# A later planned landing for the convolutions' row copies and for the preparation's read-back tile, in a four-layer state-space and attention kernel

## The chip, the cores and the metric

The kernel runs as one program on one core of a Trainium2 chip. The metric is the device time of one execution in microseconds, lower is better. A core has five engines with a queue of instructions each: TensorE (PE in the profile, its weight loads PEld), VectorE (DVE), ScalarE (ACT), GpSimd (POOL) and SyncE (SP), which here issues all DMAs. Each engine works through its queue in the order in which the program wrote it, and waits at an instruction until what it needs is there.

## The reference

Four layers on images of 64 x 64 positions with 128 channels, batch 4, all in float32.

- Layer 0 splits the channels. The left half goes through 3x3 convolutions (`c1_w`, `c2_w`) and a 1x1. The right half goes through a projection, a depthwise 3x3 convolution with SiLU, and a selective scan over four directions, 128 inner channels and 16 states. Both halves are joined by a 1x1 convolution and added to the input.
- Layer 1 is a layer norm, a projection, a depthwise 3x3 with SiLU, a selective scan with 256 inner channels (two tiles of 128), a norm, a gate, a projection, and a two-layer perceptron with GELU.
- Layer 2 is a gated message over the 3x3 neighbours, layer 3 a 7x7 neighbourhood attention with 4 heads.

The scan is the heart of layers 0 and 1:

```
xs  = four orderings of the image (rows, columns, both reversed)
dts, Bs, Cs = split(x_proj @ xs);  delta = softplus(dt_w @ dts + dt_b)
h   = exp(delta * A) * h + (delta * u) * B      # for each of 16 states
y   = sum over states of h * C, plus D * xs
```

## The kernel before

**Units.** The scans of layers 0 and 1 are cut into 3072 units in a row (4 images of layer 0 with one channel tile, 4 images of layer 1 with two; 256 units a task; 16 units make a step, which is 1024 positions of one direction). A unit holds 8 channels by 16 states on 128 partitions. For one unit SP loads `h` from the DRAM tile `dud` (512 KB, 10 units ahead, L443), PE spreads delta over the states into the PSUM tile `da` and ACT takes its exponential (`decay`, L459), and DVE runs the scan (L476). DVE also multiplies by B for two units at a time, POOL multiplies by C (L457), and PE sums over the states (`add_up`, L557). `da` has two buffers, `h` nine pairs.

**Preparation.** `Scans.prepare` (L339) makes a step's delta, `dud`, B and C, starting 28 units ahead. For a first channel tile PE computes the projection into `xd`, and SP stores it to `xdd`. For the second channel tile of layer 1 (64 of 192 steps) the projection is the same, so `xd` is read back from `xdd` with two DMAs (L378). Then come two pairs of matmul from `xd` and ACT work (L391 on), exponential, logarithm, four operations on POOL, two casts on ACT, the store of `dud`, 12 copies `dp<-parts` and the load of `repC`.

**Side work.** `Side` does all that lies around the scans: `pre0` and `pre1` (projections and the depthwise convolution), `convs`, `post0` and `post1` (output stages). The depthwise convolution (`depthwise`, L813) works in 8 pieces; a piece's rows are three DMAs into one of two `pad` tiles, started when the piece before has issued its first third of matmuls. `conv` (L850) loads two halves of the image at its start and uses them in order. Each DMA group comes with a memset of the image's border on POOL. Both are loaded through `halves` (L801), which notes a time of landing.

**The planner.** Preparation and side work are generators that yield after every small piece, with the engines that the next piece needs and, where it needs a DMA, the planned time of its landing. The program is written out unit by unit (`Scans.run`, L584). At each unit the planner's clock is the unit's number times 3.6 us (`UNIT`), and a lane's next piece is written into the engines' queues if `Lane.fits` (L188) says so:

```python
            start = max(plan.at[kind], self.ready)
            ...
            if start + USUAL[what] > plan.now + UNIT + SLACK[kind] + more:
                return False
```

`ready` is the landing time, `USUAL` is 1.4 us for PE and `SLACK` 1.2. `more` is 0.06 us for each credit that side work has saved up (at most 50; it earns at least 0.83 a unit, more when a deadline is near). A preparation piece that has fallen 4 units behind is written without asking, as is side work whose deadline is reached. Nothing of this is time on the chip: it only sets the order in the queues. Spare time on PE is filled with matmuls on zeros (`fill`, L559).

**What the change touches.** `ROWS_LANDING` is read in `halves`, for the depthwise rows and the convolutions' rows alike:

```python
        def start(n):
            pad = self.pads[n % 2]
            load(pad, n)
            tiles.append((pad, self.nc.now + ROWS_LANDING))
```

`LANDING` is read for the read-back (L379), for the store of `xd` before `repC` (L373), for the fetches of chunks and for the reuse of stored tiles.

Of the kernel before, what the change touches and what calls it, by code (L numbers as in the profile page):

```python
# [36 lines left out]
def image(t):  # L37
    return t.rearrange("p (r w) -> p r w", w=HW)
# [74 lines left out]
SLACK = dict(PE=1.2, ACT=2.2, POOL=3.0)  # L113
LANDING = 10.0
FOUR_LANDING = 14.0
ROWS_LANDING = 18.0


class Plan:
# [22 lines left out]
    def post(self, chain, issue, due=0.0):  # L142

        if self.running:
            self.posted.append((chain, max(self.done, due), issue))
        else:
            issue()
# [78 lines left out]
class ScanWeights:  # L226
# [27 lines left out]
    def load(self):  # L254

        nct, most = self.nct, max(TILES)
        tile = self.pool.tile([P, most * ND * (H + P)], F32, name="xpdt", tag="xpdt", bufs=1)
        self.xp = tile[:, 0 : nct * ND * H].rearrange("p (t k h) -> p t k h", t=nct, k=ND)
        at = most * ND * H
        self.dtw = tile[:, at : at + ND * nct * P].rearrange("p (k c) -> p k c", k=ND)  # L260
        self.nc.sync.dma_start(out=self.xp, in_=self.d_xp)
        for i in range(HALVES):
            self.nc.sync.dma_start(out=self.dtw[i * H : (i + 1) * H], in_=self.d_dtw)
# [22 lines left out]
class Scans:  # L286
# [19 lines left out]
    @staticmethod  # L306
    def half(i):
        return slice(i * T, (i + 1) * T)
# [30 lines left out]
    def prepare(self, t, step):  # L339

        nc, W, half, post = self.plan, t.W, self.half, self.plan.post
        begin = self.plan.now
        k, c = t.steps[step]
        R = W.rank
        rows = R + 2 * NS
        if t.first is None:
            yield "PE" if W.nct > 1 else "PE ACT"

        xd = self.xds[step % 2]
        if t.first is None:  # L350
            xdd = t.xdd[step] = self.dram.tile(
                [rows, TS], F32, name="xdd", tag=f"xdd{W.layer}", bufs=(4, 2 * len(t.steps))[W.layer]
            )
            ps = self.bank()
            for ti in range(W.nct):
                for i in range(HALVES):
                    nc.tensor.matmul(
                        image(ps[i * H : (i + 1) * H, :]),
                        W.xp[:, ti, k, :],
                        self.view(t.xc[ti], k, c, i, HALVES),  # L360
                        start=ti == 0,
                        stop=ti == W.nct - 1,
                    )
                if ti + 1 < W.nct:
                    yield "PE ACT" if ti + 2 == W.nct else "PE"
            nc.scalar.copy(xd, ps)

            def store_xd():
                for i in range(HALVES):
                    nc.sync.dma_start(out=xdd[:, half(i)], in_=xd[i * H : i * H + rows, :])  # L370

            post("prep", store_xd)
            ready = max(self.plan.done, self.plan.now) + LANDING  # L373
            yield "PE ACT"
        else:
            xdd, ready = t.first.xdd[step], begin
            for i in range(HALVES):
                nc.sync.dma_start(out=xd[i * H : i * H + rows, :], in_=xdd[:, half(i)])  # L378
            yield "PE ACT", self.plan.now + LANDING  # L379
        out = t.prepared[step] = {"xd": xd}  # L380

        def repeat():
            out["C"] = self.tile("repC", 2)
            src = bass.AP(xdd.tensor, xdd.offset + (R + NS) * TS, [[TS, NS], [0, 8], [1, TS]])
            nc.sync.dma_start(out=out["C"], in_=src)

        post("rep", repeat, max(begin + 15 * UNIT, ready))

        bias = W.dtb[:, k, t.ct : t.ct + 1]
        delta, low = self.tile("delta", 1), self.tile("low", 1)  # L390
        for i in range(HALVES):  # L391
            ps = self.bank()
            nc.tensor.matmul(
                ps,
                W.dtw[i * H : (i + 1) * H, k, t.ct * P : (t.ct + 1) * P],
                xd[i * H : (i + 1) * H, :],
                start=True,
                stop=True,
            )
            nc.scalar.activation(low[:, half(i)], ps, AF.Abs, bias=bias)  # L400
            nc.scalar.activation(delta[:, half(i)], ps, AF.Relu, bias=bias)
            yield "PE ACT" if i + 1 < HALVES else "ACT"
        nc.scalar.activation(low, low, AF.Exp, scale=-1.0)
        yield "ACT"
        nc.scalar.activation(low, low, AF.Ln, bias=1.0)
        yield "POOL"
        nc.gpsimd.tensor_add(delta, delta, low)
        yield "ACT POOL"
        parts = self.tile("parts", 1, shape=(P, 3, TS), dtype=BF16)
        nc.scalar.copy(parts[:, 0, :], delta)  # L410
        nc.gpsimd.tensor_mul(image(low), image(delta), self.view(t.xc[t.ct], k, c, 0, 1))
        yield "POOL"
        t.x_done = step == len(t.steps) - 1
        dud = out["du"] = self.dram.tile([P, TS], F32, name="dud", tag="dud", bufs=3)
        post("prep", lambda: nc.sync.dma_start(out=dud, in_=low))
        nc.gpsimd.tensor_sub(delta, delta, parts[:, 0, :])
        yield "ACT"
        nc.scalar.copy(parts[:, 1, :], delta)
        yield "POOL"
        nc.gpsimd.tensor_sub(parts[:, 2, :], delta, parts[:, 1, :])  # L420


        def own(part, j):
            if j == part == 0:
                out["delta"] = self.dps[step % 2]
            nc.sync.dma_start(
                out=out["delta"][32 * part : 32 * part + 32, j, :], in_=parts[32 * j : 32 * j + 32, part, :]
            )

        for i in range(12):  # L430
            j, part = divmod(i, 3)
            post("rep", lambda part=part, j=j: own(part, j), begin + (11 + 0.5 * i) * UNIT)
        yield ""
# [221 lines left out]
class Side:  # L655
# [145 lines left out]
    def halves(self, load):  # L801
# [3 lines left out]
# [5 lines that stand above are left out]
# [1399 lines left out]
```

## Time and profile before

| | us |
|---|---|
| median of 3 runs | 13472.44 |
| lowest, highest | 13461.69, 13475.99 |
| the profiled execution | 13484.91 |
| its span, first to last instruction | 13483.1 |
| stretch of the scans (207 to 11213) | 11006 |
| behind the scans (layers 2 and 3) | 2270 |

The profile is of one execution. Its page gives the busy time of each engine, the span in 40 slices, the DMA queues, and the costliest groups of instructions, each with the idle time of its engine just before it and who ended that. Further views give who waited for whom (total, times, longest), the busy times in a stretch, and the instructions in order of time. `L102` is the planner's wrapper, through which all of the preparation's and side work's instructions go, so these are told apart by the tile they write: `ms` is the one PSUM bank of preparation and side work, `pad` the convolutions' rows, `xd` the preparation's tile. The granted TensorE clock is 0.902 of full speed over the span.

### The profile page before, as it was taken

The page shows a single profiled execution, that of the slowest core. Times are in us where ns is not written, and L with a number is a line of the kernel's source. Part 1 is how long each engine was busy: PE and PEld are TensorE (multiplying, and loading weights), DVE is VectorE, ACT ScalarE, POOL GpSimd, SP SyncE. Part 2 cuts the span into 40 slices and gives each one's busy share as a digit, 9 for nine tenths or more (in the row PEclk, how much of TensorE's full clock was granted, in tenths as well). Part 3 has the DMA queues.
Part 4 walks back from the last instruction along what each step waited for, and adds up shares of the span by engine and source line. Part 5 has one row for each costly group of instructions (what it writes and reads, how often), then busy time and mean ns, then how long its engine had stood idle before and what let it go on. Part 6 is the DMA issues. An engine that isn't in the chain of part 4 may idle for free. (4 is left out here: it accounts for less than half of the span.)

```text
span 13483.1 us, 129941 instructions
## 1 busy us (share of the span) xinstructions
PE 9508.7 (71%) x41730; PEld 2802.6 (21%) x42299; DVE 11700.5 (87%) x6988; ACT 7918.1 (59%) x10594; POOL 9716.6 (72%) x3218
## 2 busy tenths in 40 slices
PE   5776777667667776767766677677777676665788
PEld 1111111111111111111111111122112122111455
DVE  4998999989999889989999999999999992677555
ACT  3666556655665556655665555555555554655577
POOL 3887788878887778778888888888888883345200
PEclk8888999989898889989999899999999988877899
DMA  6888888898888888998889888888888882344200
GB/s 157 215 211 219 222 212 214 223 219 219 198 227 206 208 208 211 221 216 215 204 218 220 219 196 199 200 197 213 202 201 201 197 194 73 84 99 104 65 20 17
DMA packets 877394, 2476.31 MB, mean 184 GB/s; under 512 B 142495, under 2 KB 164135, under 8 KB 868519
## 3 DMA queue, kind: packets, MB, share of 16 engines
q1 hardware_dynamic: 876711, 2467.95, 74.0%
q8 instruction: 337, 5.52, 0.2%
q14 instruction: 346, 2.83, 0.1%
HBM read 2044.11 MB, written 272.37 MB: 172 GB/s over the span
## 5 line engine op out<-in xcount | busy, mean ns | idle before, releaser
L457 POOL TENSOR_TENSOR h<-h,repC 128x2048 f32<-128x2048 f32 x1536 | 6953.0, 4532 | 1536.4 <-ACT state L494 1199.7
L476 DVE TENSOR_TENSOR_SCAN h<-da,state,h 128x1024 f32<-128x1024 f32 x2304 | 5302.8, 2338 | 390.3 <-ACT da L467 270.9
L467 ACT ACTIVATE da<-da,av 128x1024 f32<-128x1024 f32 x3072 | 3338.7, 1088 | 3187.2 <-PE da L465 2847.7
L457 DVE TENSOR_TENSOR h<-h,B 128x2048 f32<-128x2048 f32 x1536 | 3474.6, 2262 | 282.7 <-DMA h<-dud 192.0
L465 PE MATMUL da<-dp,spread 128*128 128x512 bf16 x5753 | 1915.1, 411 | 2253.8 <-DVE h L476 2188.2
L557 PE MATMUL yps<-h,gather 128*32 128x512 f32 x12288 | 1866.2, 683 | 17.6 <-issue 3.8
L476 DVE TENSOR_TENSOR_SCAN h<-da,h 128x1024 f32<-128x1024 f32 x768 | 1722.2, 2279 | 128.0 <-ACT da L467 89.8
L562 PE MATMUL yps<-ones,nothing 128*128 128x512 bf16 x4943 | 1438.4, 403 | 32.9 <-issue 28.1
L465 PEld LDWEIGHTS <-spread 128*128 128x128 bf16 x6144 | 553.0, 101 | 4176.2 <-issue 3656.9
L102 ACT ACT_TABLE_LOAD x600 | 769.8, 1283 | 18.3 <-DMA xcd<-o 5.0
L562 PEld LDWEIGHTS <-nothing 128*128 128x128 bf16 x5121 | 457.0, 101 | 1413.1 <-issue 1092.3
L102 PE MATMUL ms<-d,wts 128*128 128x512 f32 (+3 forms) x900 | 547.5, 717 | 253.8 <-POOL d L102 106.4
L102 POOL TENSOR_TENSOR delta<-delta,low 128x1024 f32<-128x1024 f32 x192 | 451.8, 2353 | 312.2 <-ACT low L102 231.0
L102 ACT CAST parts<-delta 128x1024 bf16<-128x1024 f32 x384 | 400.7, 1044 | 440.4 <-POOL delta L102 415.1
L1919 POOL COPY wide_total<-total 128x128 f32<-128x128 f32 x128 | 37.6, 294 | 831.7 <-DVE total L1917 650.8
L102 PE MATMUL ms<-xd,xpdt 64*128 64x512 f32 x768 | 470.3, 694 | 231.6 <-ACT delta L102 82.4
L540 PE MATMUL yps<-y,ident 128*128 128x512 f32 x576 | 483.9, 928 | 78.2 <-ACT y L574 73.7
L102 POOL TENSOR_TENSOR low<-delta,xc 128x1024 f32<-128x1024 f32 x192 | 503.3, 2622 | 8.9
L1475 ACT ACTIVATE hid<-hid,relb 128x1024 f32<-128x1024 f32 x288 | 322.8, 1146 | 271.2 <-DVE hid L1470 271.0
L1888 ACT ACTIVATE s<-s,least 128x512 f32<-128x512 f32 x512 | 372.2, 727 | 178.9 <-DVE least L1875 178.9
L1875 DVE CUSTOM_DVE_ANT_0 s<-sps,bias 128x512 f32<-128x512 f32 x512 | 323.5, 687 | 173.6 <-PE sps L1864 165.0
L1577 POOL TENSOR_TENSOR acc<-acc,part 128x1024 f32<-128x1024 f32 x120 | 309.4, 2584 | 221.3 <-DVE part L1571 134.5
(291 smaller groups left out, 11191.4 us busy)
## 6 DMA issues: line engine op xcount, KB each, us to landing
h<-dud SPq DMA_DIRECT2D x3072, 512.0 KB
dp<-parts SPq DMA_DIRECT2D x2304, 64.0 KB
repC<-xdd SPq DMA_DIRECT2D x192, 512.0 KB
dud<-low SPq DMA_DIRECT2D x192, 512.0 KB
spread<-gd SPq DMA_DIRECT2D x72, 1024.0 KB
pad<-xid SPq DMA_DIRECT2D x192, 256.0 KB
szd<-o SPq DMA_DIRECT2D x96, 256.0 KB
xcd<-o SPq DMA_DIRECT2D x96, 256.0 KB
```

Source lines behind the costliest of these rows:

```text
L102: return call(*args, **kw)
L457: engine.tensor_mul(pair, pair, t.prepared[step][name].unsqueeze(1).to_broadcast([P, 2, TS]))
L465: self.nc.tensor.matmul(da[:, cols], self.C.spread[:, jj, :], dp[:, j, cols], start=True, stop=True)
L467: self.nc.scalar.activation(da, da, AF.Exp, scale=t.W.a[:, at : at + 1])
L476: nc.vector.tensor_tensor_scan(h[:, way], da[:, way], h[:, way], 0.0 if step % NSTEP == 0 else t.states[step - 1][:, u % NG : u % NG + 1], ...
L540: self.nc.tensor.matmul(self.like_part(yps, k), self.C.ident, self.part(t.y, k, c, b), start=True, stop=False)
L557: self.nc.tensor.matmul(out, self.C.gather[jj], rhs, start=False, stop=jj == 3)
L562: self.nc.tensor.matmul(self.live["yps"], self.C.nothing, self.C.ones16, start=False, stop=False, skip_group_check=True)
L1475: nc.scalar.activation(hid, hid, AF.Gelu, bias=self.relb[:, m, t : t + 1])
L1577: (nc.vector if alone and pair else nc.gpsimd).tensor_add(acc, acc, part)
L1875: self.nc.vector.tensor_tensor_reduce(out=self.live["s", n][:, h, :], in0=self.live["sps", n][:, h, :], in1=self.bias[case][:, h, :], scal ...
L1888: self.nc.scalar.activation(s, s, AF.Exp, scale=-1.0, bias=self.live["least", n][:, h : h + 1], accum_out=self.live["total", n][:, h : h + 1],
```

## The change

The planned landing of the convolutions' rows goes from 18 to 27 us after they are issued, and the planned landing of the read-back `xd` gets a constant of its own, 16 us instead of the common 10. What is computed, in which instructions and on which engine, stays as it is; the places of side work and preparation in the queues change, and with them the number of filling matmuls.

```diff
@@ -113,7 +113,8 @@
 SLACK = dict(PE=1.2, ACT=2.2, POOL=3.0)
 LANDING = 10.0
 FOUR_LANDING = 14.0
-ROWS_LANDING = 18.0
+ROWS_LANDING = 27.0
+AGAIN_LANDING = 16.0
 
 
 class Plan:
@@ -376,7 +377,7 @@
             xdd, ready = t.first.xdd[step], begin
             for i in range(HALVES):
                 nc.sync.dma_start(out=xd[i * H : i * H + rows, :], in_=xdd[:, half(i)])
-            yield "PE ACT", self.plan.now + LANDING
+            yield "PE ACT", self.plan.now + AGAIN_LANDING
         out = t.prepared[step] = {"xd": xd}
```

## The prediction

> **What bounds the kernel now.** I read the busy shares first, then the stretch with the scans alone, then DVE's waits and PE's waits in that stretch, then the timeline of one stall.
>
> ```profile
> PE 9508.7 (71%) x41730; PEld 2802.6 (21%) x42299; DVE 11700.5 (87%) x6988; ACT 7918.1 (59%) x10594; POOL 9716.6 (72%) x3218
> ```
>
> ```profile
> 207.00:11213.00 11006.00, 7779.81 (x30865) 2012.66 (x31437) 10390.05 (x4619) 6472.52 (x8005) 9055.94 (x2732) 0.91 0.85 210
> ```
>
> The columns of the second are length, then busy time of PE, PEld, DVE, ACT, POOL, then clock, DMA share and GB/s. The 3072 scan units take 11006 of 13483 us, 3.58 us each. DVE is busy 10390 us of it (94%), POOL 9056 (82%), PE 7780 (71%). So DVE bounds this stretch, and what can be won without touching DVE's own work is its idle time, 616 us. Gaps under 0.15 us make up 152 us of it (the pipeline's own); 464 us are real waits.
>
> ```profile
> DVE h L476 <- ACT da L467: 360.7, 221, 10.9
> DVE h L457 <- issue: 61.4, 30, 15.2
> DVE h L457 <- PE B L502: 15.6, 13, 5.3
> ```
>
> Columns: total us, times, longest. A scan waits for its decay factors `da`, which ACT makes from a PE matmul. What made PE late is in PE's own waits of the same stretch:
>
> ```profile
> PE da L465 <- DVE h L476: 2188.2, 1303, 10.6
> PE ms L102 <- DMA pad<-xid: 104.7, 21, 11.0
> PE ms L102 <- DMA xd<-xdd: 54.1, 13, 10.6
> PE ms L102 <- DMA pad<-ld: 45.6, 6, 13.8
> PE ms L102 <- DMA dp<-parts: 4.4, 2, 2.9
> ```
>
> The first row is PE waiting for DVE to free a `da` bank, which is harmless. The other four are side or preparation matmuls (`ms`) standing in PE's queue before their tile has landed. The two rows named `dp` are tap matmuls too. In all 208.8 us in 42 waits. While PE stands there, the `da` matmuls behind it wait:
>
> ```profile
> 2976.10 3.73 SPq L799 DMA_DIRECT2D pad<-ld  x4
> ...
> 2993.74 3.66 PE L102 MATMUL ms<-pad,wts 128*64 128x512 f32 x8 [13.80 <-DMA pad<-ld]
> ...
> 2998.40 1.09 ACT L467 ACTIVATE da<-da,av 128x1024 f32<-128x1024 f32 x1 [16.11 <-remote]
> ...
> 2999.53 2.29 DVE L457 TENSOR_TENSOR h<-h,B 128x2048 f32<-128x2048 f32 x1 [15.23 <-issue]
> ```
>
> The convolution's rows are issued at 2976, PE stands 13.8 us until they land, ACT's `da` is 16 us late, DVE loses 15.2 us. Of each such PE wait I added up DVE's gaps (over 0.15 us) in the 12 us after it: pads 149 us of DVE idle after 155 us of PE waits (0.96), `xd` read-backs 43.5 after 54.1 (0.80). So 193 us of DVE's 464 hang on these two landings, and DVE, being the bound, gets them back one for one.
>
> **The change, part by part.** No instruction's work changes; two constants move where the planner puts steps in the queues. A step enters a queue when its start is no later than now + 3.6 + 1.2 - 1.4 us for PE, up to 3 us more with credit. For rows 18 - 3.4 = 14.6 us gives 4 units at least, 27 - 3.4 = 23.6 gives 7, or 6 with credit. For the read-back 10 - 3.4 = 6.6 gives 2 units, 16 - 3.4 = 12.6 gives 4.
>
> *Rows of the convolutions (104 loads beside the scans).* Working the planner's arithmetic through both programs, the tap stands behind its load by 4 units (33 depthwise loads), 5 (17), 6 (17), 7 to 9 (21); after the change 6 (53), 7 (30), 8 (5). The first load of each of the 8 convolutions goes from 4 to 6; their second loads stand 13 units or more behind either way and never waited. A unit is 3.58 us, so the shortest cover grows by 7.2 us. For every load I took the trace's slack (PE's arrival at the first tap minus the landing) and added the change of distance times 3.58: waits of 156.6 us become 38. The wait of 13.8 above keeps 6.5, one of 8.0 at 1055 keeps 0.7, and all below 5 go. Saved: 118 x 0.96 = 113 us of DVE.
>
> *The read-back of `xd` (64 steps, second tile of layer 1).* Distances 2 units (42), 3 (14), 4 and more (8) become 4 (48), 5 (6), 6 (10). The 13 waits less 7.2 us each leave 10.6 - 7.2, 10.0 - 7.2, 8.7 - 7.2: 8 of 54. Saved: 46 x 0.80 = 37 us.
>
> *Steps that move behind these.* All later steps of a read-back preparation move by 2 units: the two matmul pairs, the exponential and logarithm on ACT, four POOL operations, two casts, and the store of `dud`. The store is planned on average 10 to 11 units after the start and its first reader (`h` load, on SP's queue) 18 after, so some 7 units, 25 us, still cover it. The copies `dp<-parts` and `repC` keep their place: they are held in one chain until unit 15 or 16, before as after. On SP the row loads keep their distance from the taps that trigger them; nothing is added to a queue, and POOL's padding memsets move with their loads. Fill matmuls go from 5547 to 5639 by the planner's count: 92 x 0.40 us on PE, under the 2188 us that PE waits for DVE; uncovered they would cost 37.
>
> *What gets tighter.* A depthwise pass now takes 6 to 7 units a piece in place of 4 to 7, so the stages with it last longer (layer 1's projection of image 0: 203 units to 231, of image 2: 217 to 246) and the stages behind are packed: the output stage of layer 0, image 3, from 136 units to 111, the first of layer 1 from 333 to 294. No step is forced by a deadline in either program. The trace has no row for the packed stages, so I bound them: DVE's idle outside the waits above is about 0.07 us a unit. Sorting units by how far the planner has PE or ACT booked, and applying the after program's booking, gives -24 us by PE and +14 us by ACT. I take +10, near the upper end since packing adds ACT work; the ends -24 and +14 go into the range.
>
> *Sum.* -113 - 37 + 10 = -140 us. The profiled execution took 13484.9 us (span 13483.1), 12.5 above the median of the runs, 13472.4. 13484.9 - 140 = 13345; taken to the median, 13332. I say **13335**.
>
> *A rule of the Trainium skill beside it.* Taps took 592 ns at the median, but 1054 ns each just after the 13.8 us wait above. The Trainium skill, TensorE: Matmul & The Clock Gate, section "What's actually happening", says that PE's clock halves after an idle window of about 3.4 us and returns after as long a busy one; the trace agrees with the halving. By that page each of the some 22 waits over 3.4 us costs, as an estimate, another 1.7 us (half of 3.4), and the sum would be 37 us better. By the rows it is in the 0.96 already, since DVE's gap counts what follows the wait.
>
> **The rivals.**
>
> *Half the gain.* What a load needs is not constant: measured from PE's arrival at its own unit, landings came 0 to 28.7 us later, because SP issued them up to 28 us behind the plan (its `h` loads wait for PE's sums for 2227 us in this stretch). Six units are 21.5 us. If later loads meet SP as late as the worst quarter did, half of the waits come back: -70, **13402**. For: the long waits come in clusters where a stall delays SP. Against: the same stalls cause the lateness, and they shrink.
>
> *Slower.* The packed stages become the loss: between units 434 and 2343, where side work is densest, ACT and PE run late often enough to starve the scan. The densest stage of the trace (output stage of image 2, units 1263 to 1362) idles DVE 0.18 us a unit beside DMA waits, against 0.07. 1909 units x 0.11 = +210, less 150: **13532**. It decides from +0.08 us a unit on, more than double today's idle. Against: only two or three stages are packed by over 10%, and the longer passes are thinner.
>
> *No use.* DVE's stalls turn into waits for POOL, whose products feed PE's sums and so free the `h` buffers: then some 20 us remain, **13450**. Against: POOL idles 1950 us in the stretch and DVE's waits for POOL add up to under 15.
>
> *More.* Without the stalls PE keeps its clock, SP runs on time, and waits that I left standing (46 us), and smaller ones behind them, go as well: all 193 us, **13280**. The Trainium skill's clock page named above would point this way.
>
> **How the numbers follow.** Forecast 0.57, half 0.18, more 0.10, slower 0.10, no use 0.05. A measurement here tells about 0.2% (27 us) from no change. Faster: 0.57 + 0.18 + 0.10 = 0.85. Same: 0.05. Slower: 0.10. From "more" (13280) to past "half" (13402), with the ends of the packing (-24 and +14) and the uncovered fills (37) at the slow end: 13275 to 13440. That leaves out 0.15.
>
> **What would show it.** Right: PE's waits on `pad` fall from about 155 to under 50 us and on `xd` from 54 to about 10; DVE's waits on `da` from 361 to some 220; the stretch of scans from 11006 to about 10865; the stretch behind it unchanged at 2270. Half: pad waits stay near 80. Slower: DVE's waits for ACT `da` grow in stages without row loads, with PE waiting there on ACT's `d`, `sq` or `o`. No use: DVE's row against POOL or `h<-dud` grows. Wrong altogether: the waits fall and the scans' stretch doesn't, or a read-back preparation ends so late that DVE waits on `h` at a step's start.

## The result: a quarter of the gain

| | before | after |
|---|---|---|
| median of 9 runs, us | 13478.67 | 13441.06 |
| lowest to highest | 13461.69 to 13505.85 | 13419.15 to 13461.08 |
| ratio, 95% interval | | 0.9972 [0.9962, 0.9982] |
| span of the profiled execution | 13483.1 | 13459.1 |

The change makes the kernel 0.28% faster, 38 us, where 140 were forecast; 13441 lies one microsecond past the slow end of the range. The profiled execution after (13461.08) is the slowest of its nine, so its trace shows 24 of the 38 us.

The profile after, busy shares of the page, and then the stretch of the scans (length; busy time of PE, PEld, DVE, ACT, POOL; clock, DMA share, GB/s):

```profile
PE 9585.4 (71%) x41820; PEld 2820.9 (21%) x42392; DVE 11709.6 (87%) x6988; ACT 7920.8 (59%) x10594; POOL 9722.8 (72%) x3218
```

```profile
207.00:11197.00 10990.00, 7863.55 (x30963) 2034.35 (x31534) 10395.94 (x4619) 6474.11 (x8005) 9058.89 (x2732) 0.91 0.85 210
```

The stretch is 16 us shorter (11006 before), DVE's work in it the same within 6 us, the part behind it 2262 us (2270). Among all traces of this document that part, in which no kernel differs, takes 2251 to 2270 us, so by it alone two single traces can differ by 19 us. Now PE's waits in that stretch (total us, times, longest):

```profile
PE da L466 <- DVE h L477: 2170.6, 1266, 10.1
...
PE ms L102 <- DMA pad<-xid: 32.4, 11, 7.6
...
PE ms L102 <- DMA pad<-ld: 20.3, 3, 9.7
...
PE ms L102 <- DMA dp<-parts: 19.0, 1, 19.0
...
PE ms L102 <- DMA xd<-xdd: 8.7, 3, 5.4
```

The waits that the change is about fell as forecast: `pad` from 150.3 to 52.7 us, `xd` from 54.1 to 8.7. And DVE's waits:

```profile
DVE h L477 <- ACT da L468: 309.4, 258, 18.2
DVE h L458 <- DMA h<-dud: 43.8, 12, 12.6
DVE h L458 <- issue: 33.9, 31, 3.5
DVE h L458 <- POOL delta L102: 20.4, 8, 7.9
```

They fell far less. The scan's waits for `da` went from 360.7 to 309.4 us (forecast 220), but from 221 to 258 in number, and the rows of `h<-dud` and of POOL's `delta`, 7.1 and 3.7 us before, are new in size. Of the 43.8 us of `h<-dud`, 27.6 follow within 12 us on a PE wait for rows: the longest, 12.6 us at unit 816, the first of a step, comes behind the 9.7 us that PE stood for `pad<-ld`. The sorting below counts these with the rows.

To see what took the place of what, every gap of DVE over 0.15 us in the scans' stretch was sorted by a DMA wait that lies in the 12 us before it: PE's taps on their rows, PE's matmuls on the read-back, ACT's waits for the store that must read a tile before it is written again, any other DMA that side work or preparation waited for, or none. DVE's own waits for `h` make no class; where nothing else stood before them, they are in the last column (some 5 us before, 11 after). All later sorted numbers come from this; the expectations below, written earlier, use a coarser one, in which a whole neighbourhood of units goes to a PE wait and what is left ("beside") was 232 us before and 324 after.

| us of DVE idle | all | rows | read-back | stores | other DMA | no DMA |
|---|---|---|---|---|---|---|
| before | 463.8 | 145.8 | 43.5 | 26.0 | 24.1 | 224.4 |
| after | 442.2 | 57.3 | 7.5 | 38.5 | 26.2 | 312.7 |
| difference | -21.6 | -88.5 | -36.0 | +12.5 | +2.1 | +88.3 |

So 124 us were won at the two landings, and 103 were given back elsewhere, 88 of them where no DMA is waited for. A part of the loss can be seen singly. The timeline of the changed kernel around its longest new stall (start, length, instruction; in brackets the idle time before and who ended it):

```profile
6102.57 2.13 POOL L102 TENSOR_TENSOR parts<-delta,parts 128x1024 bf16<-128x1024 f32 x1
...
6105.45 1.12 PE L102 MATMUL ms<-xd,xpdt 64*128 64x512 f32 x2
...
6108.74 0.34 SPq L416 DMA_DIRECT2D dud<-low  x1
6111.58 16.20 SPq L427 DMA_DIRECT2D dp<-parts  x12
6124.79 0.69 ACT L102 ACTIVATE low<-ms,av 128x512 f32<-128x512 f32 x1 [19.15 <-DMA dud<-low]
...
6125.95 1.09 ACT L468 ACTIVATE da<-da,av 128x1024 f32<-128x1024 f32 x1
...
6126.11 2.07 PE L102 MATMUL ms<-xd,xpdt 64*128 64x512 f32 x2 [19.00 <-DMA dp<-parts]
6127.07 2.35 DVE L477 TENSOR_TENSOR_SCAN h<-da,state,h 128x1024 f32<-128x1024 f32 x1 [18.16 <-ACT da L468]
```

A preparation ended its last POOL operation at 6104.7; the next one, whose projection had just run (`ms<-xc`), had its first matmul from `xd` done at 6106.6. ACT then stood 19 us before `low`, because the store `dud<-low` that reads the one `low` tile was issued only at 6108.7 and landed at 6124.7; `da` stood behind it in ACT's queue, and DVE lost 18.2 us. The row `PE ms <- DMA dp<-parts` above is this stall too, since PE waited for ACT to empty the bank; it is not a read-back. For this tile the planner has no landing time at all.

### The profile page after: what moved, and what is told of

Same layout as the page of the kernel before. It is cut to its first block, busy times and chain, and to the rows that moved or that the text cites. A ratio compares the mean times of both kernels' runs of the same rounds, so it can differ in the third digit from the quotient of the medians.

```text
span 13459.1 us, 130166 instructions
## 1 busy us (share of the span) xinstructions
PE 9585.4 (71%) x41820; PEld 2820.9 (21%) x42392; DVE 11709.6 (87%) x6988; ACT 7920.8 (59%) x10594; POOL 9722.8 (72%) x3218
## 5 line engine op out<-in xcount | busy, mean ns | idle before, releaser
L563 PE MATMUL yps<-ones,nothing 128*128 128x512 bf16 x5035 | 1466.4, 403 | 32.2 <-issue 26.1
```

The costliest lines, as they stand in the source:

```text
L563: self.nc.tensor.matmul(self.live["yps"], self.C.nothing, self.C.ones16, start=False, stop=False, skip_group_check=True)
```

## The experiments

The theory after the result: the landings did what was forecast, and the loss comes from how the planner packs side work. Rivals: that the read-back's part or the rows' part simply doesn't work; that longer depthwise passes push work into denser stages (pace); that they let side work save up credit, which loosens the fit for what comes after. A last rival, "reshuffle" in the expectations, is that the plan before is one of many alike, and that any other order of the pieces costs DVE about as much.

### Each part alone

```diff
 # rows_only: after, with
-AGAIN_LANDING = 16.0
+AGAIN_LANDING = 10.0
 # again_only: after, with
-ROWS_LANDING = 27.0
+ROWS_LANDING = 18.0
```

> The rows' landing at 27 us, the read-back's back at 10 us. Three theories for the DVE idle that came back (idle in gaps over 0.15 us beside the waits on DMA rose from 232 to 324 us in the scans, +92, where +10 was forecast). Packing: the longer depthwise passes squeeze the stages behind them and save up credit that loosens the fit; then most of the +92 is here: idle beside DMA waits about 300 (+70), idle behind row waits about 75 (before 167), behind read-back waits still about 45, time about 25 us under before (13455). Read-back: the 2 units by which the read-back preparations move put their pieces on top of side work; then idle beside DMA waits is about 250 (+20) and the time is about 75 us under before (13405). Reshuffle: before is one plan picked from many alike, and any other order of pieces idles DVE more; then as with packing, about 300, time about 13455, and what tells these two apart is the run with another pace.

> The read-back's landing at 16 us, the rows' back at 18 us. Packing: no depthwise pass gets longer, so idle beside DMA waits stays near 240 (before 232), the idle behind read-back waits falls from 47 to about 10, time about 30 us under before (13448). Read-back: idle beside DMA waits rises to about 290, most of it from unit 1252 on where the second tiles are prepared, and the time is 0 to 30 us over before. Reshuffle: idle beside DMA waits rises to about 290 as well, spread over the units behind 1252, time 0 to 20 us over before.

Measured: rows alone 13449.50 us, 0.9978 [0.9969, 0.9987]; the read-back alone 13484.28, 1.0004 [0.9995, 1.0013].

| us of DVE idle | all | rows | read-back | stores | other DMA | no DMA |
|---|---|---|---|---|---|---|
| rows_only | 445.2 | 50.6 | 24.2 | 36.7 | 43.1 | 290.6 |
| again_only | 455.3 | 156.3 | 1.2 | 30.5 | 45.1 | 222.2 |

The rows carry the gain and the loss: with them alone idle without a DMA is 66 us over before, with the read-back alone it is 2 below. The read-back's waits do vanish (43.5 to 1.2), but 36 us of that come back behind other DMAs, rows and stores, and the time is that of before. So by its idle this run came out as "packing" expected and by its time as the other two theories did. What the rows' landing costs also repeats from plan to plan: in units 456 to 1024 the idle without a DMA is 92.7 us after and 88.6 with the rows alone, against 36.5 before and 24.7 with the read-back alone.

### Is it how densely side work is paced?

```diff
 # pace_088_before and pace_078_before: before, with
-PACE = 0.83
+PACE = 0.88     # 0.78 in the other
```

> The kernel before with the side work's least rate at 0.88 pieces a unit in place of 0.83: both landings as before, only the order of pieces shuffled. Packing: side work is not packed behind the depthwise passes more than before, idle beside DMA waits stays within 20 us of 232 and the time within 30 us of before. Reshuffle: idle beside DMA waits rises by 50 us or more (to 280 or more), idle behind row and read-back waits stays about 215 in sum, and the time is 50 us or more over before (13530).

> The kernel before with the side work's least rate at 0.78 in place of 0.83: a second shuffle that leaves both landings alone. Packing: within 20 us of idle and 30 us of time, as before. Reshuffle: idle beside DMA waits 280 or more, time 50 us or more over before (13530).

Measured: 0.88 gives 13550.75 us, 1.0054 [1.0038, 1.0069]; 0.78 gives 13491.71, 1.0011 [1.0000, 1.0021]. Idle without a DMA is 278.9 us with 0.88 and 238.8 with 0.78. Earning credit faster costs 73 us with no landing changed, so density or credit can do harm of this size; earning it slower gains nothing. PACE moves both at once, so it doesn't tell them apart. The first run came out as "reshuffle" expected (50 us or more), the second as "packing" did (within 30 us), so the pair decides nothing between these two, and "reshuffle" stays open.

### The depthwise rows or the convolutions' rows?

```diff
 # conv_rows_only: after, with
-    def halves(self, load):
+    def halves(self, load, landing=ROWS_LANDING):
-            tiles.append((pad, self.nc.now + ROWS_LANDING))
+            tiles.append((pad, self.nc.now + landing))
 # in depthwise
-        tiles, start = self.halves(load)
+        tiles, start = self.halves(load, 18.0)
```

> The rows' landing at 27 us for the convolutions alone, the depthwise rows back at 18 us; the read-back at 16 us as after. Packing: no depthwise pass gets longer; idle beside DMA waits is about 255 us, idle behind row waits falls only by the convolutions' part (167 to about 125), behind read-back waits it is under 10, and the time is 50 us under before (13428). Rival, the longer distance itself: eight places only are moved, so it expects the same here.

Measured: 13456.92 us, 0.9984 [0.9975, 0.9993]. The depthwise passes stay short here, and units 456 to 1024 stay quiet (28.6 us without a DMA, 36.5 before): the loss there comes with the depthwise rows, not with the convolutions' rows. The waits on rows are nearly those of before (140.2 against 145.8), since the depthwise loads make most of them. The gain is less than half of the 50 us expected, and its trace doesn't show where it comes from: DVE's idle in the stretch is 460.2 us against 463.8.

### Credit alone

The planner's credit (earned by the unit, spent by the piece, at most 50) loosens the fit by 0.06 us each. In a longer depthwise pass side work can't spend it: by the planner's own count the mean credit at a side piece goes from 23 to 42 in the depthwise pass of layer 1, image 0, and from 23 to 45 in the convolutions behind it. These two kernels change the use of credit and no landing.

```diff
 # loose_fit_before: before, with
-                if not late and (credit < 1.0 or not lane.fits(0.06 * credit)):
+                if not late and (credit < 1.0 or not lane.fits(0.06 * max(credit, 30.0))):
 # tight_fit_before: before, with
+                if not late and (credit < 1.0 or not lane.fits(0.06 * min(credit, 20.0))):
```

> The kernel before, both landings as they were, but the side work's fit is never tighter than with 30 credits (1.8 us of slack more, where before has 3 to 28 credits behind unit 434). Packing by credit: this alone brings the loss without any later landing: idle beside DMA waits rises from 232 to about 310, all of it behind unit 434, and the time is 70 us over before (13548). Packing by length (only the longer passes and the fewer units left for the rest matter): idle beside DMA waits stays within 20 us of 232 and the time within 25 us of before.

> The kernel before, but credit above 20 loosens the fit no further (1.2 us at most, where before has 40 to 50 credits up to unit 434 and between 1150 and 1263). Packing by credit: idle beside DMA waits falls in the units up to 434 from 62 to about 40 us and in all to about 205, time 20 to 30 us under before (13450). Packing by length: the first stages take longer with the tight fit and push the rest together, idle beside DMA waits rises to about 260 and the time by 20 us (13500).

Measured: loose 13613.60 us, 1.0102 [1.0087, 1.0117], twice the 70 us expected; tight 13429.69, 0.9968 [0.9954, 0.9982], 46 us where 20 to 30 were expected. PE's waits in the scans' stretch of the loose kernel:

```profile
PE ms L102 <- ACT delta L102: 219.8, 177, 11.2
PE ms L102 <- DMA pad<-xid: 131.2, 20, 16.2
PE ms L102 <- POOL d L102: 105.8, 51, 6.6
PE ms L102 <- ACT o L102: 103.5, 83, 3.2
```

Before, these rows are 171.4, 104.7, 60.0 and 86.8 us: a piece written before its inputs are there stands in PE's queue for ACT, POOL and DMAs alike. Idle without a DMA goes from 224.4 to 370.4. So credit alone makes both kinds of stall; it lets a piece be written up to 3 us further ahead of its planned landing, and so it also eats into the landing times that the change lengthens.

### The change with credit held down

```diff
 # tight_fit_after: after, with
-                if not late and (credit < 1.0 or not lane.fits(0.06 * credit)):
+                if not late and (credit < 1.0 or not lane.fits(0.06 * min(credit, 20.0))):
 # conv_rows_tight: conv_rows_only, with the same line
```

> The kernel after, with credit above 20 loosening the fit no further (as in the tight fit of the kernel before, which came out 0.32% faster by itself, with 238 us of idle beside DMA waits). Loose fit (the depthwise pieces' longer landing saves up credit, and the credit brought the 92 us back): the tight fit gives them back, idle beside DMA waits is about 235 us, behind row waits about 60, behind read-back waits under 20, and the time is about 110 us under before (13366). Rival, length (a tight fit and longer passes both push side work back until its end is packed, and it is the packing that costs): idle beside DMA waits rises behind unit 2049 from 74 to 130 us or more and stays above 300 in all; the time is at most 50 us under before (13426).

> The convolutions' rows at 27 us, the depthwise rows at 18, the read-back at 16, and the tight fit. Loose fit: the gains of the convolutions' rows (0.16%) and of the tight fit (0.32%) add up, 65 us under before (13411), idle beside DMA waits about 240, behind row waits about 100. Rival, length: the two do not add up, 45 us under before at most.

Measured: 13370.98 us, 0.9926 [0.9913, 0.9938] for the first; 13456.51, 0.9986 [0.9977, 0.9996] for the second. The stretch of the scans of the first, up to 11109 (its last scan ends at 11112, so the whole is 10905 us long), and its PE waits:

```profile
207.00:11109.00 10902.00, 7907.53 (x31412) 2030.65 (x31412) 10388.10 (x4619) 6473.24 (x8005) 9055.89 (x2732) 0.91 0.86 212
```

```profile
PE ms L102 <- ACT delta L102: 219.7, 207, 6.2
...
PE ms L102 <- DMA xd<-xdd: 35.1, 7, 10.4
...
PE da L466 <- DMA pad<-ld: 2.6, 1, 2.6
```

| us of DVE idle | all | rows | read-back | stores | other DMA | no DMA |
|---|---|---|---|---|---|---|
| tight_fit_before | 423.5 | 101.5 | 32.0 | 27.1 | 45.8 | 217.1 |
| tight_fit_after | 362.7 | 0.0 | 37.4 | 7.9 | 39.6 | 277.8 |
| conv_rows_tight | 427.3 | 104.3 | 11.7 | 41.3 | 46.8 | 223.2 |

The first came out at the time expected: 70 us below the changed kernel, nearly twice the gain of the change itself. The same bound won 46 us on the kernel before, so only some 24 of the 70 go with the later landings. No matmul of side work waits for rows any more. By the planner's arithmetic the bound moves the taps of the depthwise rows from 6 units behind their load (53 loads), 7 (30) and 8 (5) to 7 (60) and 8 (28): that they stood at 6 was the credit's doing, and with 7 the 57 us that remained are gone. The read-back is a miss: 37.4 us are back, where under 20 were expected, though its landing is still 16 us. In the projection and the depthwise pass of layer 1, image 0, idle beside DMA waits was 7.2 us before and 38.1 after; here it is 5.9. In the same stage of image 2 it is the other way round: some 3 us before, 20 after and 33 with credit bounded. Over all stages idle without a DMA falls only from 312.7 to 277.8 (by the coarse sorting from 324 to 294, where some 235 were expected): credit explains at most 35 of the 88 us, and of the 53 left nothing is settled. So the time is that of "loose fit", and the idle is nearly that of its rival, "length" (above 300). The second missed: with the convolutions' rows alone the bound on credit wins nothing over conv_rows_only (0.9984), though on the kernel before it won 0.32%. The parts don't add up.

### What is next in line behind the rows

A third tile for the depthwise rows, each piece loaded two ahead, takes the waits on rows away by another road.

```diff
 # third_rows_tile: after, with
+        pads = pads or self.pads
-            pad = self.pads[n % 2]
+            pad = pads[n % len(pads)]
 # in depthwise
-        diag = self.tile("diag", "big", (P, 12, n))
+        diag = self.tile("diag", "wts", (P, 1280))[:, 0 : 12 * n].rearrange("p (a c) -> p a c", a=12)
+        third = self.tile("third", "big", (P, 4, T)).rearrange("p i (r w) -> p (i r) w", w=HW)
+        nc.gpsimd.memset(third[96:P], 0.0)
-        tiles, start = self.halves(load)
+        tiles, start = self.halves(load, self.pads + [third])
+        start(1)
-            pad, landed = tiles.pop()
+            pad, landed = tiles.pop(0)
-                if dx == 1 and m + 1 < 8:
-                    start(m + 1)
+                if dx == 1 and m + 2 < 8:
+                    start(m + 2)
 # third_tile_late_store: this, with
-            self.free[tag] = max(self.nc.done, self.nc.now) + LANDING
+            self.free[tag] = max(self.nc.done, self.nc.now) + 20.0
 # third_tile_store_tight: that, with min(credit, 20.0) in the fit
```

> Both constants as after the change, and the depthwise convolution gets a third tile for its rows (its bytes lie in the wide tile that is free then), so that a piece's rows are loaded two pieces ahead in place of one. The taps stand 8 units and more behind their rows, but no piece waits for the planner's landing any more, so the passes are not longer than before. Packing (the longer passes save up credit, and what comes behind is fitted in more loosely and more densely): idle beside DMA waits is about 250 us (before 232, after 324), idle behind row waits about 40 (the convolutions' share), and the time is 90 to 110 us under before (13375). Rival, the longer distance itself (any plan in which the taps stand later than before meets other pieces, longer passes or not): idle beside DMA waits stays about 320, the time is 40 to 60 us under before (13430).

> The third rows tile once more, with the planned landing of the stores at 20 us in place of 10. With the rows ahead, the depthwise pieces waited for the store that frees their output tile (ACT for the store of xcd: 47 us in 7 waits, the longest 14 us, a row that neither kernel has among its longest). Next landing: these waits go, idle beside DMA waits falls from about 377 (that trace lacks 8 of DVE's records, 18 us of its 395) to about 320, and the time from 0.30% to about 0.6% under before (13395). Rival, loose fit alone: the 47 us are ACT's and mostly hidden; idle beside DMA waits stays within 20 us of 377, the time within 25 us of the run with the third tile.

> The third rows tile, the stores' landing at 20 us and the tight fit together, both constants as after. Loose fit: row and read-back waits under 30 us, idle beside DMA waits about 240, the fastest of all, 150 us under before (13326). Rival, length: side work ends as late as with the tight fit of before (planned end 3044 in both), so no packing is added, but the other waits that a fuller plan brings keep idle beside DMA waits at about 300; 80 us under before (13396).

Measured: 13432.02 us, 0.9970 [0.9958, 0.9983]; 13409.27, 0.9951 [0.9937, 0.9964]; 13376.78, 0.9925 [0.9911, 0.9939].

| us of DVE idle | all | rows | read-back | stores | other DMA | no DMA |
|---|---|---|---|---|---|---|
| third_rows_tile | 453.3 | 16.9 | 0.0 | 82.5 | 49.5 | 304.4 |
| third_tile_late_store | 414.4 | 12.5 | 20.6 | 104.1 | 31.1 | 246.1 |
| third_tile_store_tight | 383.5 | 10.2 | 13.2 | 51.9 | 51.3 | 256.9 |

Of each of these three gains, 17 us are won ahead of the scans. Image 0's depthwise pass runs before them and loads its rows two ahead as well; PE's waits on rows there fall from 31.3 us before to 14.6 with the third tile, and DVE's first multiplication by B starts at 187 us in place of 203 to 206. From that multiplication to the last scan the third tile's kernel takes 11004 us, the changed kernel 10994 and the kernel before 11008. (The expectation of the second run takes eight DVE records of the first's trace for missing; all 6988 are there, and seven of them lie before 207 us, where the counting begins.)

The first came out as its rival expected (13430, idle beside DMA waits about as after the change), and not as "packing" did (13375). Its depthwise pass of layer 1, image 0, is as short as before (92 units; 108 after the change), and by the planner's count the mean credit there is 28, nearly the 23 of before. Yet idle without a DMA is 304.4 us, and in the projection and depthwise pass of that image it is still some 26 us (7.2 before, 38.1 after the change). So the longer passes and the credit that they save up are not the whole cause of the 88 us.

The waits on rows and read-back are nearly gone, and yet the scans take 10 us longer than in the changed kernel. ACT's waits in the third tile's kernel show what stands there instead:

```profile
ACT L102 <- DMA xcd<-o: 47.2, 7, 14.1
ACT low L102 <- DMA dud<-low: 21.3, 3, 10.8
ACT o L102 <- DMA xcd<-o: 20.4, 4, 13.4
```

Depthwise pieces now follow so closely that ACT comes to the output tile `o` before its store has landed: 67.6 us in these rows, 8.3 before the change. The planned landing of that store was the next suspect, and here the explanation fell although the kernel became faster: with 20 us in place of 10, the two rows of `xcd<-o` are 48.1 and 47.4 us, more than without. What fell was the idle without a DMA (304.4 to 246.1). In the longest wait of the third tile's kernel ACT stood from 1036.1, the store was issued at 1037.3 and landed at 1050.1; in the longest of the next, ACT stood from 2948.4 and the store was issued at 2949.6. There the issue on SP was late, not only the landing, and a later planned landing doesn't mend that; what held SP back wasn't followed further. Only the bound on credit brought the rows of `xcd<-o` down, to 16.5 and 2.7 us. That last kernel was expected at 13326, or at 13396 by its rival, and came out nearer to the rival. It is no faster than tight_fit_after without a third tile (13370.98), and here the bound leaves idle without a DMA no lower (256.9 against 246.1).

## Why the prediction was wrong

*What bounds the kernel*: right. DVE's work in the scans' stretch is 10390 us before, 10396 after and 10391 with the bound on credit, and the time follows its idle: between before and tight_fit_after idle falls by 101 us, the stretch by 101, the median of nine runs before and that of the bounded kernel differ by 108.

*Rows*, forecast -113: measured -88.5. The distances in units are those of the sum, the sixes among them. What was left was too small in it: 38 us of PE waits and some 36 us of DVE idle were forecast, 52.7 and 57.3 measured. In the trace of the change PE came to each of the 14 taps that still waited 1 to 17 us after the last issue of their rows, where 6 units are 21.5 us. So SP had issued them late, as the rival "half the gain" names. With a seventh unit between, no row wait is left.

*Read-back*, forecast -37: measured -36.0 in the trace of the change, in part by luck. Alone it gave -42 in its own waits and nothing in time, which the sum, adding one term to the next, could not show. With credit bounded 37.4 of the 43.5 us of before are back at the same landing. In the 7 waits of that trace PE came to the matmul between 7.7 us ahead of the read-back's second issue and 1.9 us behind it, where the plan has at least 4 units, 14.3 us, between. What the constant of 16 us has to cover is SP's lateness, and that differs from plan to plan.

*Steps that move behind these*, forecast at nothing: the store of `dud` was looked at for its reader `h` and not for the next writer of `low`. ACT's waits on it went from 8.8 to 33.0 us of DVE idle; its rows before and after are:

```profile
ACT low L102 <- DMA dud<-low: 11.4, 2, 9.9
ACT low L102 <- DMA dud<-low: 36.3, 4, 19.1
```

As rows_only has 30.1, they come with the rows' plan and not with the read-back, whose move they were to be charged to. Together with the stores of `o`, `ld` and others the term is +12.5.

*What gets tighter*, forecast +10 with the ends -24 and +14: this is the step that failed. Idle without a DMA rose by 88.3 us. The bounds came from sorting units of before by how far PE and ACT were booked and applying the bookings of after. That gave a narrow pair of ends, and it left out the one quantity that the longer passes change most, the saved-up credit, although the text had it in the fit. Bounding the credit takes back 35 us of it at most; what makes the other 53 stays open. A wider bound was at hand in the rival "slower", whose price of 0.11 us a unit came from the densest stage.

*The rival "slower"* had its place right and its price near: from unit 456 to 2049 idle without a DMA rose from 106.1 to 204.4 us, 0.062 a unit, against the 0.08 from which it decides. It took most of the gain and not all. Its reason, density, is only partly right: in layer 1, image 0, the pass became longer and thinner, and it is there that idle grew by 31 us, until credit was bounded.

*"No use"* had its sign come partly true: DVE's row against POOL's `delta` grew to 20.4 us and `h<-dud` to 43.8, from 10.8 together. That is 53 us more, but most of `h<-dud` follows on waits for rows, and with credit bounded, where no row wait is left, it is 4.6 us. So POOL was not what took the gain. *"More"* did not come; the granted clock was 0.902 before and 0.899 after. By the clock rule of the Trainium skill, TensorE: Matmul & The Clock Gate, "What's actually happening", the prediction had estimated another 37 us for the some 22 waits; no run here shows such a surplus.

*The range* has a slip in its sum: 13402 with the 37 us of fills is 13439 already, so the slow end of 13440 has no room for the +14 that it names too.

Of the signs named, `xd` to about 10 (8.7) and the part behind the scans unchanged (2262) came true, pads to under 50 (52.7) was just missed, and `da` to 220 (309.4) and the stretch to 10865 (10990) did not come. What did come is near to the sign of "wrong altogether": the waits fell and the scans' stretch, but for 16 us, didn't. Of the +88 us, 53 stay open. In units 1252 to 2049 idle without a DMA is 90.0 us after, 87.6 with credit bounded, 76.6 in the bounded kernel before, where no landing is changed, and some 50 before; plans that differ in nothing but order differ by this much there, and no run tells why. The rival "reshuffle" is not excluded for this part.

## What to carry to other kernels

When a step in an in-order queue is planned to land later, price the waits that it removes and then everything that the planner does with the slack: saved credit, tolerances and due times loosen or tighten the order of work far from the edit. Here 103 of 124 us came back, a part of it by saved credit and half of it unexplained. Look also at when the transfer is really issued: here the waits that stayed were for copies that SP had issued units later than planned. A wait taken away uncovers the next landing that is planned too early or not at all (the store of `o`, the store of `low`), so look at every reuse of a tile behind the moved step, its next writer as well as its next reader. A sum over stalls holds only as long as the order of the rest is kept; where a planner rewrites it, the spread between plans that should be equal is the smallest error that a forecast can claim.

## What the runs showed of the hardware

The longest new stall came from a store (19.1 us of ACT) and not from a load (the longest wait on rows before was 13.8 us of PE): `dud<-low` (512 KB) took 16.0 us from issue to landing at 6108.7, `xcd<-o` (256 KB) 12.8 us at 1037.3, while the DMA engines were 85% and 84% busy in the stretch. The twelve `dp<-parts` issues behind the first took SP's queue 16.2 us, 1.35 us each, so one burst of small copies is as long as such a landing. The same read-back `xd<-xdd` landed 2.1 us after its issue at 4733.6 and 7.6 us after it at 7334.5, and PE came to the matmul 0.6 us before its second issue the first time and 1.8 us after it the second. No single constant fits both.
